# A second residual buffer with rows loaded and biased ahead, and the second norm's rows of thirteen blocks turned on VectorE through DRAM, in a conditioned transformer block

## The chip, the cores and the metric

The kernel runs on one core of one Trainium2 chip. The metric is the device time of one execution in microseconds; a kernel's time is the median of its runs. A profile describes one execution, and its span is a little shorter than that execution's own time.

## The reference, cut to what matters

One transformer block on x (8 x 1024 x 512, fp32), with 16 heads of 32 and an MLP of width 2048. A condition vector for each batch element gives the shifts, scales and gates of the two halves.

```python
mod = silu(condition) @ Wada + bada
sh_a, sc_a, gt_a, sh_m, sc_m, gt_m = jnp.split(mod, 6, axis=1)
xn = _layernorm(x, g1, be1)
xm = xn * (1.0 + sc_a[:, None, :]) + sh_a[:, None, :]
x = x + gt_a[:, None, :] * _attention(xm, Wqkv, Wproj, bproj)   # causal softmax
xn = _layernorm(x, g2, be2)
xm = xn * (1.0 + sc_m[:, None, :]) + sh_m[:, None, :]
h = gelu(xm @ W1 + b1)
x = x + gt_m[:, None, :] * (h @ W2 + b2)
```

## The kernel before

**Blocks and windows.** The tokens are cut into 16 blocks of 512, two for each batch element; block n is the first half of its sequence where n is even and the second, whose queries see twice as many keys, where it is odd. The program is a sequence of windows. In window w TensorE does the attention of block w (scores of four heads at a time, their maxima, exponentials, weights times values) and beside it the "linear" steps that the dictionary `plan` (L231 to L269) lists for that window: the output projection, second norm and MLP of block w-1 (`proj`, `mt`, eight parts `u` and `d`), the v projection of block w, the k and q projections of block w+1, and the loading, first norm and transposition of block w+2 (`load_xa`, `norm_a`, `at`).

**Who decides the order.** All of it is settled while the program is built. A planner keeps estimated times (`now`, `due`, `written`) for each engine and each tile; generators that stand for the linear steps yield what they need, and the planner picks at each point (`work` L1343, `step_aside` L1377) whether attention or a linear step comes next. It also picks VectorE, ScalarE or GpSimd for many small operations (`either` L150, whose VectorE and GpSimd calls are L158 and L161; `combine_out` L192, whose VectorE call is L193; `sooner`). `note` adds to the estimates, and constants such as `LANDING` (10 us) and `HOLDING` (8 us) say when a DMA is expected to be done. Each engine then runs its list in order.

**Products.** The q, k, v, up and down products are seven half-size products each (Strassen-Winograd) and all pass through `matmul` (L197 to L210). Their weights come in pieces of 256 KB through a ring of `RING` = 9 buffers: `fetch` (L328) issues the next load on SyncE as soon as the piece `RING` places earlier is released, and `release` is called when a product is done with its pieces.

**Weights and scores in attention.** Scores go to a PSUM tile, the mask is added (L1531), maxima are taken (L1534), and weights go through the same PSUM tile (L1610) to the exponential (L1622). Where PSUM banks are free the scores of a group are instead made head by head in those.

**Residual rows.** Step `load_xr` (L1258 to L1270) loads the block's 512 rows of x with four DMAs of 256 KB into the one buffer of pool `xrp`; block 14 uses a buffer of the key pool. It stands in the window of that block's projection. `project_out` (L1006) queues four additions of the bias row `gba`, multiplies each projected tile by the gate row `ga`, adds it, and starts the second norm. `down` adds the row `gbm` in its part 0; `settle` adds the MLP's result; `store` (L1100) issues two DMAs of 256 KB for each half block as soon as the last addition is planned, so that SyncE waits at them. `gate_broadcasts` (L508) loads all four rows once for each batch element, each into a tile of its own.

**Norms.** `normalize` (L573) takes statistics on VectorE (L583, L584), makes the reciprocal root and the offset on GpSimd (L605 to L608) and applies them on VectorE or ScalarE (L619, L624) into the tile `hat`, of which there is one. `normalize_tile` (L632) does the same tile by tile in the last block. `modulated` (L685) brings the rows into the transposed layout `xm` and applies gain and shift (L732 VectorE, L738 ScalarE), and then makes sums for Strassen (L746, L748). There are two ways, picked by the set `by_pe` (L375): 16 transposes on TensorE (L728) into PSUM; or `turn` (L656), in which VectorE transposes 32 x 32 squares in four passes (L664), one DMA writes the 1 MB to DRAM (L673), four DMAs read it back with the squares in their places (L678) into `hat`, and the gain and shift read SBUF. Both DMAs are on SyncE's queue, which also carries every weight load; the read-back is issued behind the write and waits until it has landed. Before, all 16 second norms and the first norms of blocks 0 and 1 go through TensorE, and the other 14 first norms are turned.

Of the kernel before, what the change touches and what calls it, by code (L numbers as in the profile page):

```python
# [9 lines left out]
F32 = mybir.dt.float32  # L10
# [12 lines left out]
def kernel(  # L23
# [47 lines left out]
    HB = D // 2  # L71
    RING = 9

# [3 lines left out]
    act = ctx.enter_context(tc.tile_pool(name="act", bufs=2))  # L77
    xrp = ctx.enter_context(tc.tile_pool(name="xrp", bufs=1))
    pp = ctx.enter_context(tc.tile_pool(name="pp", bufs=1))
# [148 lines left out]
    def mlp_steps(n):  # L228
# [6 lines left out]
        0: [("load_xa", 2), ("preps",), ("k", 1), ("norm_a", 2), ("gates", "a"), ("q", 1)]  # L235
        + [("mod", 3), ("at", 2), ("v", 1), ("mod", 4), ("columns_m",), ("gates", "m")],
    }
    late = []
    for w in range(1, NB):
        n = w - 1  # L240
        m = mlp_steps(n)
        even = blocks[n][1] == 0
        rows_a = [("rows", blocks[n][0], "a")] if even else []
        rows_m = [("rows", blocks[n][0], "m")] if even else []
        own = m[:1] + ([("load_xa", w + 2)] if w + 2 < NB else []) + m[1:3]
        own += [("norm_a", w + 2)] if w + 2 < NB else []
        if w == NB - 1:
            steps = late[:1] + [("load_xr", n)] + rows_a + [("proj", n), ("mt", n)] + late[1:]
            steps += [("v", w)] + rows_m + own + m[3:6]
            late = m[6:]  # L250
        else:

            steps = late + [("v", w), ("load_xr", n)] + rows_a + [("proj", n), ("mt", n), ("k", w + 1)]
            if w == 2:
                steps = late + [("v", w), ("k", w + 1), ("load_xr", n)] + rows_a + [("proj", n), ("mt", n)]
            if w == 1:
                steps = [("load_xr", n)] + rows_a + [("k", w + 1), ("proj", n), ("mt", n)]
            steps += [("q", w + 1)] + rows_m + own
            at = [("at", w + 2)] if w + 2 < NB else []
            if blocks[w][1] == 0:  # L260

                steps += m[3:5]
                late = m[5:6] + at + m[6:]
            else:
                steps += m[3:6] + at
                late = m[6:]
        plan[w] = steps
    n = NB - 1
    plan[NB] = [("load_xr", n), late[0], ("beside", late[1]), ("proj", n), ("mt", n)] + mlp_steps(n)  # L269

# [103 lines left out]

    by_pe = {f"m{n}" for n in range(NB)} | {"a0", "a1"}  # L375
    Q = P // NTT
# [20 lines left out]
    make_identity(nc, ident)  # L397
    mask = const.tile([P, 2 * P], F32, tag="mask", name="mask")
    for i in range(2):
        make_causal_mask(nc, mask[:, ts(i, P)], MASKED)  # L400
    eps = const.tile([P, 1], F32, tag="eps", name="eps")
    nc.gpsimd.memset(eps, EPS)
    ones = const.tile([P, P], F32, tag="ones", name="ones")
    nc.gpsimd.memset(ones, 1.0)
# [586 lines left out]

    residual, stored = {}, {}
    y_count, y_keys = [0], {}
# [98 lines left out]
    def settle(n, f, t, y, ky):  # L1092
# [5 lines left out]
        add_to(residual[n][:, half(t, 2), c], y, [ky], keys)  # L1098

    def store(n, t):  # L1100
        b, h = blocks[n]
        for i in (2 * t, 2 * t + 1):
            r0 = h * TB + i * P
            nc.sync.dma_start(out[b, r0 : r0 + P, :], residual[n][:, i, :])
        stored[n + 1] = max(stored.get(n + 1, 0.0), due([("xr", n, 2 * t), ("xr", n, 2 * t + 1)]))

    def down(n, part):
# [85 lines left out]
        if part == 0:  # L1193
            yield [("g", n, 0), ("g", n, 1), "prepared"], []
            for i in range(NTT):
                add_to(residual[n][:, i, :], gate_rows["gbm"], [("row", "gbm")], [("xr", n, i)])
            combine(nc.vector, "B12", "B12", "B11")
# [47 lines left out]
    def perform(step):  # L1245
# [12 lines left out]
        elif kind == "load_xr":  # L1258
            n = step[1]
            b, h = blocks[n]  # L1260
            if n == NB - 2:
                xr = kvp.tile([P, NTT, D], F32, tag="kT", name=f"xr_{n}")
            else:
                xr = xrp.tile([P, NTT, D], F32, tag="xr", name=f"xr_{n}")
            residual[n] = xr
            for t in range(NTT):
                r0 = h * TB + t * P
                nc.sync.dma_start(xr[:, t, :], x[b, r0 : r0 + P, :])
                landed = max(now["PE"], stored.get(n, 0.0)) + LANDING + 700 * t
                written["xr", n, t] = landed  # L1270
        elif kind == "norm_a":
# [179 lines left out]
    def diagonals(parts, sc):  # L1451

        if parts[-1][4] == parts[0][4]:
            first, span = parts[0][3] - P, len(parts) * P
            return span, sc[:, :, first : first + span]
        return 2 * P, sc.rearrange("p j (a c) -> p j a c", c=2 * P)[:, :, :, P:]
# [19 lines left out]
    def scores_by_heads(n, g, parts, reads):  # L1476

        h = blocks[n][1]
        for some in (range(HPG - 1), range(HPG - 1, HPG)):
# [14 lines left out]
            for j, bank in of.items():  # L1494
                if parts[0][1] == h:
                    span, place = diagonals(parts, banks[bank].unsqueeze(1))
                    place = place[:, 0]
                    shape_of = mask[:, :span]
                    if len(place.shape) == 3:
                        shape_of = shape_of.rearrange("p (a c) -> p a c", c=P)  # L1500
                    nc.vector.tensor_tensor(place, place, shape_of, ALU.add)
# [8 lines left out]
    def scores_at_once(n, g, parts, reads):  # L1510
# [149 lines left out]
    def finish(n, g):  # L1660
# [176 lines left out]
    for n in range(NB):  # L1837
        written["attended", n] = NEVER
        written["v done", n] = NEVER
        written["m used", n] = NEVER  # L1840
        if n > 1:
# [73 lines left out]
```

## Time and profile before

| | |
|---|---|
| runs | 3565.46, 3567.45, 3569.86 us; median 3567.45 |
| the profiled execution's own time | 3568.64 us |
| its span | 3566.9 us |
| granted TensorE clock | 0.995 |
| DMA | 461.77 MB, 129 GB/s on average; the main queue holds 43.4% of the 16 engines' time |
| chain of waits | TensorE 88%, DMA 4%, GpSimd 3%, VectorE 3%, ScalarE 1% |

In the lines of the profile PE is TensorE, DVE VectorE, ACT ScalarE, POOL GpSimd and SP SyncE; "SPq" is the queue in which SyncE issues its DMAs. A line of the timeline gives the start of a run of like instructions in us, the us until its last one ends, engine, source line, operation, output<-input, shape and count, and in brackets an idle time ahead of it with what ended it. A line of groups gives the busy us of all of them and the mean ns of one, then the idle time before them. A line of waits gives the instruction that waited, what released it, the us waited in all, the number of waits and the longest. `xm_a`, `hat_a`, `held_a` are the tiles of a first norm, `xm_m`, `hat_m`, `held_m` those of a second one.

### The profile page before, as it was taken

What the parts mean: (1) busy time and instruction counts of PE and PEld (TensorE: products, weight loads), DVE (VectorE), ACT (ScalarE), POOL (GpSimd) and SP (SyncE); (2) the same over time, 40 slices, a digit from 0 to 9 for tenths busy, and PEclk for the clock granted to TensorE, in tenths of its full rate; (3) what the DMA queues carried; (4) which work ended last, traced back from release to release, by engine and by line L of the source; (5) the groups of instructions that cost most, each with busy time, mean ns of one, the idle gap of its engine ahead of it and who ended that gap; (6) DMA issues with size and microseconds to landing.
All of it is one profiled execution on the core that took longest, in us unless ns stands there. A gap on an engine that the chain in (4) does not pass through costs nothing.

```text
span 3566.9 us, 120690 instructions
## 1 busy us (share of the span) xinstructions
PE 3490.9 (98%) x54621; PEld 1741.5 (49%) x54621; DVE 2181.1 (61%) x2395; ACT 1186.3 (33%) x1229; POOL 2081.8 (58%) x2247
## 2 busy tenths in 40 slices
PE   8999999999999999999999999999999999999999
PEld 4444445444554545445454454544545445454445
DVE  6776575665746557365574665746666466665663
ACT  2334333352323514234241442323423134231521
POOL 3667746675456754577536675366762667526660
PEclk9999999999999999999999999999999999999999
DMA  6753434435453344533445334453344533434334
GB/s 201 241 179 93 141 102 127 124 108 155 113 150 107 104 154 117 158 100 101 146 121 148 105 102 146 120 151 103 103 140 126 152 103 105 143 108 142 92 111 137
DMA packets 318259, 461.77 MB, mean 129 GB/s; under 512 B 27052, under 2 KB 177388, under 8 KB 315700
## 3 DMA queue, kind: packets, MB, share of 16 engines
q1 hardware_dynamic: 317632, 454.03, 43.4%
q8 instruction: 430, 7.05, 0.8%
q14 instruction: 81, 0.66, 0.1%
q10 hardware_dynamic: 116, 0.03, 0.0%
HBM read 408.80 MB, written 43.06 MB: 127 GB/s over the span
## 4 chain that ended last, share of the span: by engine, by line
PE 88%; DMA 4%; POOL 3%; DVE 3%; ACT 1%; issue 1%; SPq 1%; ACTq 0%; DVEq 0%; POOLq 0%
PE bank L202 60%; PE sc L1517 8%; PE po L1650 7%; PE st L1610 7%; PE st L1598 3%; DMA w<-in_L_cond_Wproj_dram 2%; PE bank L1671 2%; POOL pT L1740 1%; DMA hat_a<-held_a 1%; PE bank L728 1%; DVE mx L1534 1%; POOL hT L161 1%; PE bank L1572 0%; DVE sc L1531 0%; DMA w<-in_L_cond_Wada_dram 0%
## 5 line engine op out<-in xcount | busy, mean ns | idle before, releaser
L1740 POOL TENSOR_TENSOR pT<-pT,pT 128x256 f32<-128x256 f32 (+3 forms) x1254 | 1213.2, 1003 | 336.1 <-PE po L1650 183.4
L1622 ACT ACTIVATE pT<-st 128x2048 f32<-128x2048 f32 x288 | 541.0, 1878 | 1115.0 <-PE st L1610 1032.9
L202 PE MATMUL bank<-w,hT 128*32 128x256 f32 x14336 | 813.7, 380 | 0.2 <-POOL pT L1627 0.2
L1534 DVE TENSOR_REDUCE mx<-sc 128x4 f32<-128x2048 f32 (+3 forms) x384 | 666.0, 1755 | 216.2 <-PE sc L1517 210.0
L202 PEld LDWEIGHTS bank<-w,hT 128*32 128x32 f32 x14336 | 451.6, 110 | 367.6 <-issue 82.5
L202 PE MATMUL bank<-xm_m,w 128*32 128x256 f32 x8192 | 498.4, 380 | 0.0
L202 PE MATMUL bank<-t_m,w 128*32 128x256 f32 x6144 | 383.2, 380 | 0.1
L202 PEld LDWEIGHTS bank<-xm_m,w 128*32 128x32 f32 x8192 | 256.0, 110 | 222.2 <-issue 55.5
L1627 POOL TENSOR_SCALAR_AFFINE_SELECT pT<-pT 128x512 f32<-128x512 f32 x256 | 169.0, 678 | 332.4 <-ACT pT L1622 332.2
L1517 PE MATMUL sc<-kT,qT 32*128 32x512 f32 (+3 forms) x3072 | 329.1, 520 | 2.0 <-DVE mx L1534 1.7
L1531 DVE TENSOR_TENSOR sc<-sc,mask 128x1024 f32<-128x1024 f32 (+1 forms) x160 | 162.8, 1018 | 273.5 <-PE sc L1517 187.3
L1650 PE MATMUL po<-pT,v 128*32 128x512 f32 (+3 forms) x3048 | 303.1, 493 | 2.0 <-POOL pT L1627 2.0
L1610 PE MATMUL st<-qT,kT 32*128 32x512 f32 (+3 forms) x3072 | 300.6, 487 | 0.0
L202 PEld LDWEIGHTS bank<-t_m,w 128*32 128x32 f32 x6144 | 189.4, 110 | 180.7 <-issue 57.5
L202 PE MATMUL bank<-w,qT 128*32 128x512 f32 x2048 | 244.7, 606 | 21.2 <-DMA w<-in_L_cond_Wproj_dram 19.7
L1689 DVE RECIPROCAL rec<-rec 128x128 f32<-128x128 f32 x256 | 224.5, 919 | 33.2 <-ACT rec L1680 33.2
L202 PE MATMUL bank<-xm_a,w 128*32 128x256 f32 x3968 | 244.6, 380 | 0.0
L1517 PEld LDWEIGHTS sc<-kT,qT 32*128 32x128 f32 x3072 | 129.3, 183 | 172.8 <-ACT pT L1622 63.9
L202 PE MATMUL bank<-t_a,w 128*32 128x256 f32 x2944 | 190.9, 382 | 0.4 <-ACT xm_m L738 0.4
L193 DVE TENSOR_TENSOR hT<-bank,u_u 128x512 f32<-128x512 f32 x192 | 129.3, 685 | 101.2 <-PE bank L202 99.9
L1064 ACT ACTIVATE hT<-hT,cols 128x512 f32<-128x512 f32 x256 | 164.5, 711 | 55.3 <-DVE hT L193 54.7
L202 PEld LDWEIGHTS bank<-xm_a,w 128*32 128x32 f32 x3968 | 123.5, 110 | 106.5 <-issue 30.8
(216 smaller groups left out, 3396.6 us busy)
## 6 DMA issues: line engine op xcount, KB each, us to landing
w<-in_L_cond_W_dram SPq DMA_DIRECT2D x384, 256.0 KB
w<-kept_up_S SPq DMA_DIRECT2D x256, 256.0 KB
w<-kept_down_S SPq DMA_DIRECT2D x256, 256.0 KB
w<-kept_qkv_S SPq DMA_DIRECT2D x180, 256.0 KB
w<-in_L_cond_Wqkv_dram SPq DMA_DIRECT2D x147, 256.0 KB
hat_a<-in_x_dram SPq DMA_DIRECT2D x64, 256.0 KB
w<-in_L_cond_Wproj_dram SPq DMA_DIRECT2D x64, 256.0 KB
xr<-in_x_dram SPq DMA_DIRECT2D x64, 256.0 KB
```

Source lines behind the costliest of these rows:

```text
L193: nc.vector.tensor_tensor(out, src, other, op)
L202: nc.tensor.matmul(ps[r, :], columns, rhs, start=start, stop=stop, skip_group_check=True)
L1064: nc.scalar.activation(hT[:, i, :], hT[:, i, :], AF.Gelu, bias=cols[:, O_B1 + f : O_B1 + f + 1])
L1517: nc.tensor.matmul(sc[:, j, c0 : c0 + w], qTs[n][r, gg, ts(qt, P)], keys_of(n, kh)[r, gg, :w], start=True, stop=True, skip_group_check=True,)
L1531: nc.vector.tensor_tensor(place, place, shape_of.to_broadcast(place.shape), ALU.add)
L1534: nc.vector.tensor_reduce(maxima[n, gg][:, kh, qt, :], sc[:, :, c0 : c0 + w], axis=AX.X, op=ALU.max)
L1610: nc.tensor.matmul(st[:, j, c0 : c0 + w], kT[r, gg, ts(k % NTT, P)], qT[r, gg, TB - w :], start=False, stop=True, skip_group_check=True,)
L1622: nc.scalar.activation(pT[:, :, :used], st[:, :, :used], AF.Exp, scale=scale)
L1627: nc.gpsimd.affine_select(diagonal, diagonal, pattern=[[0, HPG], [1, P]], compare_op=ALU.is_ge, fill=0.0, base=0, channel_multiplier=-1,)
L1650: nc.tensor.matmul(po[r, TB - w :], v[:, k % NTT, g * P + j * hd : g * P + (j + 1) * hd], pT[:, j, c0 : c0 + w], start=(k == 0), stop=last ...
L1689: nc.vector.reciprocal(some, some)
L1740: nc.gpsimd.tensor_tensor(into, into, pT[:, j, c0 : c0 + w], ALU.add)
```

## The change

1. The ring has 8 weight buffers and not 9, and `xrp` has two buffers. The mask is one square and not two, and the tile of ones has 32 columns; the mask addition and the column sums read them by broadcasting or whole.
2. `load_xr` of block w moves from the window of its projection to the window of its attention, behind part 0 of `d` of block w-1 (block 0: into window 0). It is a generator: it waits, in the planner's estimates, until block w-2 is stored, issues two DMAs of 512 KB, waits for the additions to block w-1, loads the bias row and queues the four bias additions. `project_out` waits until that has been done.
3. Bias rows `gba` and `gbm` are loaded for each block (`bias_row`) into one shared tile, `gbm` after the projection; `gate_broadcasts` loads the gate rows alone.
4. `store` is a generator that issues its DMA (one of 512 KB) only once the last addition is planned to be done.
5. `by_pe` keeps a0, a1, m0, m14 and m15, so that the second norms of blocks 1 to 13 go through `turn`.

```diff
-    RING = 9
+    RING = 8
...
-    xrp = ctx.enter_context(tc.tile_pool(name="xrp", bufs=1))
+    xrp = ctx.enter_context(tc.tile_pool(name="xrp", bufs=2))
...
-            steps = late + [("v", w), ("load_xr", n)] + rows_a + [("proj", n), ("mt", n), ("k", w + 1)]
+            steps = late + [("v", w)] + rows_a + [("proj", n), ("mt", n), ("k", w + 1)]
...
-                steps += m[3:5]
+                steps += m[3:5] + [("load_xr", w)]
                 late = m[5:6] + at + m[6:]
             else:
-                steps += m[3:6] + at
+                steps += m[3:5] + [("load_xr", w)] + m[5:6] + at
...
-    by_pe = {f"m{n}" for n in range(NB)} | {"a0", "a1"}
+    by_pe = {"a0", "a1", "m0", f"m{NB - 2}", f"m{NB - 1}"}
...
-    mask = const.tile([P, 2 * P], F32, tag="mask", name="mask")
-    for i in range(2):
-        make_causal_mask(nc, mask[:, ts(i, P)], MASKED)
+    mask = const.tile([P, P], F32, tag="mask", name="mask")
+    make_causal_mask(nc, mask, MASKED)
...
-    ones = const.tile([P, P], F32, tag="ones", name="ones")
+    ones = const.tile([P, hd], F32, tag="ones", name="ones")
...
-        for name in (f"g{kind}", f"gb{kind}"):
-            row = rowp.tile([P, D], F32, tag=f"row{name}", name=f"row_{name}_{b}")
-            nc.sync.dma_start(row, kept_rows[name][b : b + 1, :].to_broadcast([P, D]))
-            gate_rows[name] = row
+        name = f"g{kind}"
+        row = rowp.tile([P, D], F32, tag=f"row{name}", name=f"row_{name}_{b}")
+        nc.sync.dma_start(row, kept_rows[name][b : b + 1, :].to_broadcast([P, D]))
+        gate_rows[name] = row
+
+    def bias_row(n, kind):
+
+        b = blocks[n][0]
+        row = rowp.tile([P, D], F32, tag="rowgb", name=f"row_gb{kind}_{n}")
+        nc.sync.dma_start(row, kept_rows[f"gb{kind}"][b : b + 1, :].to_broadcast([P, D]))
+        gate_rows[f"gb{kind}"] = row
+        written["row", f"gb{kind}", n] = now["PE"] + LANDING
...
-        yield [("attended", n)], []
+        yield [("attended", n), ("xr begun", n)], []
         attT = qTs[n]
         tiles = [residual[n][:, t, :] for t in range(NTT)]
-        for t, xt in enumerate(tiles):
-            xt_job = lambda t=t, xt=xt: add_to(xt, gate_rows["gba"], [("row", "gba")], [("xr", n, t)])
-            pool_jobs.append((xt_job, [("xr", n, t)]))
...
         run_pool_jobs(True)
+        bias_row(n, "m")
...
     def store(n, t):
-        b, h = blocks[n]
-        for i in (2 * t, 2 * t + 1):
-            r0 = h * TB + i * P
-            nc.sync.dma_start(out[b, r0 : r0 + P, :], residual[n][:, i, :])
-        stored[n + 1] = max(stored.get(n + 1, 0.0), due([("xr", n, 2 * t), ("xr", n, 2 * t + 1)]))
+        unstored.setdefault(n, 2)
+
+        def when_added():
+            yield [("xr", n, 2 * t), ("xr", n, 2 * t + 1)], []
+            nc.sync.dma_start(some_rows(out, n, t), residual[n][:, half(t, 2), :])
+            unstored[n] -= 1
+            if unstored[n] == 0:
+                written["stored", n] = now["PE"]
+
+        start(when_added())
+
+    def load_xr(n):
+
+        if n > 1:
+            yield [("stored", n - 2)], []
+        xr = xrp.tile([P, NTT, D], F32, tag="xr", name=f"xr_{n}")
+        residual[n] = xr
+        for t in range(2):
+            nc.sync.dma_start(xr[:, half(t, 2), :], some_rows(x, n, t))
+        for t in range(NTT):
+            written["xr", n, t] = now["PE"] + LANDING
+        if n > 0:
+            yield [("xr", n - 1, t) for t in range(NTT)], []
+        bias_row(n, "a")
+        row = ("row", "gba", n)
+        for t in range(NTT):
+            job = lambda t=t: add_to(xr[:, t, :], gate_rows["gba"], [row], [("xr", n, t)])
+            pool_jobs.append((job, [("xr", n, t), row]))
+        written["xr begun", n] = 0.0
...
         elif kind == "load_xr":
-            n = step[1]
-            b, h = blocks[n]
-            if n == NB - 2:
-                xr = kvp.tile([P, NTT, D], F32, tag="kT", name=f"xr_{n}")
-            else:
-                xr = xrp.tile([P, NTT, D], F32, tag="xr", name=f"xr_{n}")
-            residual[n] = xr
-            for t in range(NTT):
-                r0 = h * TB + t * P
-                nc.sync.dma_start(xr[:, t, :], x[b, r0 : r0 + P, :])
-                landed = max(now["PE"], stored.get(n, 0.0)) + LANDING + 700 * t
-                written["xr", n, t] = landed
+            start(load_xr(step[1]))
...
-            shape_of = mask[:, :span].unsqueeze(1)
-            if len(place.shape) == 4:
-                shape_of = shape_of.rearrange("p o (a c) -> p o a c", c=P)
+            shape_of = mask.unsqueeze(1).unsqueeze(1)
...
-                    banks[bank][r, TB - w :], ones[:, :hd], term[:, j, c0 : c0 + w],
+                    banks[bank][r, TB - w :], ones, term[:, j, c0 : c0 + w],
```

More of the change, by code (lines that the diff above doesn't have):

```diff
@@ L235 @@
         0: [("load_xa", 2), ("preps",), ("k", 1), ("norm_a", 2), ("gates", "a"), ("q", 1)]
-        + [("mod", 3), ("at", 2), ("v", 1), ("mod", 4), ("columns_m",), ("gates", "m")],
+        + [("mod", 3), ("at", 2), ("v", 1), ("load_xr", 0), ("mod", 4), ("columns_m",), ("gates", "m")],
     }
@@ L247 @@
         if w == NB - 1:
-            steps = late[:1] + [("load_xr", n)] + rows_a + [("proj", n), ("mt", n)] + late[1:]
-            steps += [("v", w)] + rows_m + own + m[3:6]
+            steps = late[:1] + rows_a + [("proj", n), ("mt", n)] + late[1:]
+            steps += [("v", w)] + rows_m + own + m[3:5] + [("load_xr", w)] + m[5:6]
             late = m[6:]
         else:
-            steps = late + [("v", w), ("load_xr", n)] + rows_a + [("proj", n), ("mt", n), ("k", w + 1)]
+            steps = late + [("v", w)] + rows_a + [("proj", n), ("mt", n), ("k", w + 1)]
             if w == 2:
-                steps = late + [("v", w), ("k", w + 1), ("load_xr", n)] + rows_a + [("proj", n), ("mt", n)]
+                steps = late + [("v", w), ("k", w + 1)] + rows_a + [("proj", n), ("mt", n)]
             if w == 1:
-                steps = [("load_xr", n)] + rows_a + [("k", w + 1), ("proj", n), ("mt", n)]
+                steps = rows_a + [("k", w + 1), ("proj", n), ("mt", n)]
             steps += [("q", w + 1)] + rows_m + own
@@ L268 @@
     n = NB - 1
-    plan[NB] = [("load_xr", n), late[0], ("beside", late[1]), ("proj", n), ("mt", n)] + mlp_steps(n)
+    plan[NB] = [late[0], ("beside", late[1]), ("proj", n), ("mt", n)] + mlp_steps(n)
     kept_sums = {}
@@ L990, in move_v @@
         vs[n] = v
-    residual, stored = {}, {}
+    residual = {}
     y_count, y_keys = [0], {}
@@ L1098, in settle, with some_rows @@
         add_to(residual[n][:, half(t, 2), c], y, [ky], keys)
-    def store(n, t):
-        b, h = blocks[n]
-        for i in (2 * t, 2 * t + 1):
-            r0 = h * TB + i * P
-            nc.sync.dma_start(out[b, r0 : r0 + P, :], residual[n][:, i, :])
-        stored[n + 1] = max(stored.get(n + 1, 0.0), due([("xr", n, 2 * t), ("xr", n, 2 * t + 1)]))
+    unstored = {}
+    def some_rows(of, n, t):
+        b, h = blocks[n]
+        rows = of[b, h * TB + 2 * t * P : h * TB + (2 * t + 2) * P, :]
+        return rows.rearrange("(t p) d -> p t d", p=P)
+    def store(n, t):
+        unstored.setdefault(n, 2)
[23 more added lines that the diff above has]
+        written["xr begun", n] = 0.0
     def down(n, part):
@@ L1193, in down @@
         if part == 0:
-            yield [("g", n, 0), ("g", n, 1), "prepared"], []
+            yield [("g", n, 0), ("g", n, 1), "prepared", ("row", "gbm", n)], []
             for i in range(NTT):
-                add_to(residual[n][:, i, :], gate_rows["gbm"], [("row", "gbm")], [("xr", n, i)])
+                add_to(residual[n][:, i, :], gate_rows["gbm"], [("row", "gbm", n)], [("xr", n, i)])
             combine(nc.vector, "B12", "B12", "B11")
@@ L1454, in diagonals @@
             first, span = parts[0][3] - P, len(parts) * P
-            return span, sc[:, :, first : first + span]
+            return span, sc[:, :, first : first + span].rearrange("p j (a c) -> p j a c", c=P)
         return 2 * P, sc.rearrange("p j (a c) -> p j a c", c=2 * P)[:, :, :, P:]
@@ L1497, in scores_by_heads @@
                     place = place[:, 0]
-                    shape_of = mask[:, :span]
-                    if len(place.shape) == 3:
-                        shape_of = shape_of.rearrange("p (a c) -> p a c", c=P)
+                    shape_of = mask.unsqueeze(1).to_broadcast(place.shape)
                     nc.vector.tensor_tensor(place, place, shape_of, ALU.add)
@@ L1839 @@
         written["v done", n] = NEVER
+        written["stored", n] = NEVER
+        written["xr begun", n] = NEVER
         written["m used", n] = NEVER
```

## The prediction

> **What bounds the kernel now.** I read the page's busy times first, then TensorE's own waits in the steady part (500 to 3200 us), then SyncE's waits, then the timeline around the steps that the change touches.
>
> ```profile
> span 3566.9 us, 120690 instructions
> PE 3490.9 (98%) x54621; PEld 1741.5 (49%) x54621; DVE 2181.1 (61%) x2395; ACT 1186.3 (33%) x1229; POOL 2081.8 (58%) x2247
> ...
> PE bank L202 <- DMA w<-in_L_cond_Wproj_dram: 19.7, 14, 3.1
> PE bank L202 <- DVE v L193: 5.2, 3, 2.1
> ...
> SPq L1104 <- POOL xr L161: 80.5, 23, 9.0
> ```
>
> TensorE is busy 98% of the span and no other engine passes 61%. So time can come off only by taking instructions from TensorE or by ending its few waits: in the steady part 19.7 us go to pieces of Wproj that land late and 5.2 us to one VectorE step. SyncE stands 80.5 us at output stores whose last addition is not done. That blocks weight loads behind it, but only what shows up as a TensorE wait costs time. A kernel this full also loses time one for one whenever TensorE runs out of work. That is the question of this change.
>
> **The transposes that go.** Block 5's, between two pieces of a projection:
>
> ```profile
> 1316.37 1.06 PE L202 MATMUL bank<-w,qT 128*32 128x512 f32 x8
> 1317.25 1.91 PE L202 MATMUL bank<-xm_a,w 128*32 128x256 f32 x32
> ...
> 1354.08 0.55 PE L728 MATMUL bank<-ident,hat_m 128*128 128x128 f32 x3
> 1354.55 0.64 PE L202 MATMUL bank<-t_a,w 128*32 128x256 f32 x8
> 1355.12 0.76 PE L728 MATMUL bank<-ident,hat_m 128*128 128x128 f32 x5
> 1355.82 1.07 PE L202 MATMUL bank<-t_a,w 128*32 128x256 f32 x16
> 1356.82 1.09 PE L728 MATMUL bank<-ident,hat_m 128*128 128x128 f32 x8
> 1357.84 0.64 PE L202 MATMUL bank<-t_a,w 128*32 128x256 f32 x8
> 1358.35 1.93 PE L202 MATMUL bank<-xm_m,w 128*32 128x256 f32 x32
> 1360.10 1.26 PE L202 MATMUL bank<-t_m,w 128*32 128x256 f32 x20
> ...
> L728 PE MATMUL bank<-ident,hat_m 128*128 128x128 f32 x256 | 44.0, 295 | 4.5 <-ACT hat_m L651 3.4 <-ACT hat_m L624 1.0
> ```
>
> From 1354.08 to 1358.35 pass 4.27 us. In them stand 32 matmuls of a projection, which take 1360.10 - 1358.35 = 1.75 us on their own, so the 16 transposes cost 2.52 us, changes of form included. Thirteen blocks: 13 x 2.52 = 32.8 us. Bounds: the run of eight takes 1357.84 - 1356.82 = 1.02 us, which gives 208 x 0.128 = 27 us; the busy time of the group gives 208 x 44.0 / 256 = 36 us. I take 33 us off. All of it is on the path.
>
> **What comes in on VectorE.** 52 transposes of 32x32 squares, like the first norm's:
>
> ```profile
> L664 DVE STREAM_TRANSPOSE xm_a<-hat_a 128x512 f32<-128x512 f32 x56 | 34.6, 671 | 0.0
> ```
>
> 52 x 0.671 = 34.9 us on an engine that is 39% idle. The gain and shift stay 64 passes, now mostly from SBUF. I cost both at nothing by themselves; the cover is VectorE's idle time. VectorE works in order, though: behind a turn that waits for its rows stand the score maxima, and TensorE's next scores wait for those. I price this inside the next part.
>
> **What comes in as latency.** A turned block cannot start its first MLP product until its rows have gone to DRAM and back. The same route for the first norm, at three places, and its best halves at two:
>
> ```profile
> 125.67 2.43 DVE L664 STREAM_TRANSPOSE xm_a<-hat_a 128x512 f32<-128x512 f32 x4
> 129.23 1.46 SPq L673 DMA_DIRECT2D held_a<-xm_a  x1
> 134.78 3.43 SPq L678 DMA_DIRECT2D hat_a<-held_a  x4
> 144.49 2.91 ACT L738 ACTIVATE xm_a<-hat_a,shifta,gaina 128x512 f32<-128x512 f32 x4
> ...
> 1269.78 2.42 DVE L664 STREAM_TRANSPOSE xm_a<-hat_a 128x512 f32<-128x512 f32 x4
> 1291.67 2.22 ACT L738 ACTIVATE xm_a<-hat_a,shifta,gaina 128x512 f32<-128x512 f32 x3 [3.78 <-DMA hat_a<-held_a]
> ...
> 1703.63 2.42 DVE L664 STREAM_TRANSPOSE xm_a<-hat_a 128x512 f32<-128x512 f32 x4
> 1728.92 2.23 ACT L738 ACTIVATE xm_a<-hat_a,shifta,gaina 128x512 f32<-128x512 f32 x3 [6.96 <-DMA hat_a<-held_a]
> ...
> 2375.30 2.88 SPq L678 DMA_DIRECT2D hat_a<-held_a  x4
> 2383.80 0.82 ACT L738 ACTIVATE xm_a<-hat_a,shifta,gaina 128x512 f32<-128x512 f32 x1 [7.16 <-DMA hat_a<-held_a]
> ```
>
> From the turn's end to the first use: 144.49 - 128.10 = 16.4 us, 1291.67 - 1272.20 = 19.5 us, 1728.92 - 1706.05 = 22.9 us. The best halves, 134.78 - 129.23 = 5.6 out and 2383.80 - 2375.30 = 8.5 back, make 14.1. One modulation (0.8 us of the last row) follows before the first product can start. So 14.9 to 23.7 us. The first norm's trips share the DMA engines with the output stores and the residual loads; the second norm's fall between the projection and the MLP, where only weights move. I take 18, nearer the fast row.
>
> What covers it is TensorE's work between the output projection and the first MLP product. In block 5 the projection ends at 1317.25 and that product starts at 1358.35: 41.1 us. I counted the same stretch in the order of the built programs: 1.75 us a projection piece, the attention groups by their rows. For before this gives 41.6 in block 5, 0.5 too much. For after, W is that work, and E the end of the VectorE turn, both from the end of the output projection. E follows from the place of the turn in VectorE's order. In block 5 it stands behind the fourth product of the q projection:
>
> ```profile
> 1347.36 0.68 DVE L193 TENSOR_TENSOR u_q<-bank,u_q 128x512 f32<-128x512 f32 x1
> ...
> 1342.55 0.20 POOL L608 TENSOR_TENSOR offset_m<-offset_m,rstd_m 128x4 f32<-128x4 f32 x1
> ```
>
> That sum came 1347.36 - 1317.25 = 30.1 us after the projection; by the count of after it is 29.2, then 0.7 for itself and 2.4 for the turn, with the waits between them 32.6. The norm's own scalars (L608, 25.3 us after the projection) are in time for it. All thirteen, in us:
>
> ```
> block    1    2    3    4    5    6    7    8    9   10   11   12   13
> W     29.2 52.7 46.8 46.4 43.6 41.4 42.5 40.1 39.0 42.4 40.2 35.5 40.2
> E     23.7 36.7 39.0 28.2 32.6 19.7 29.1 23.2 20.0 28.2 24.7 19.7 30.3
> idle  12.5  2.0 10.2  0.0  7.0  0.0  4.6  1.1  0.0  3.8  2.5  2.2  8.1
> ```
>
> Idle is E + 18 - W where positive; together 54 us. With 16 it is 35, with 14.9 about 28, with 23.7 some 122. W already holds attention work brought forward: in eleven of the blocks only scores and weights stand between the last q product and the MLP, up to six scores in block 3. Such a stretch cannot run at TensorE's pace:
>
> ```profile
> 1523.77 1.14 PE L1517 MATMUL sc<-kT,qT 32*128 32x512 f32 x8
> ...
> 1528.77 2.29 DVE L1534 TENSOR_REDUCE mx<-sc 128x4 f32<-128x2048 f32 x1 [0.31 <-PE sc L1517]
> 1349.16 1.88 ACT L1622 ACTIVATE pT<-st 128x2048 f32<-128x2048 f32 x1 [2.19 <-PE st L1610]
> ```
>
> Scores and weights share one PSUM tile, so each score holds it for 1.1 us of TensorE and then 2.3 us of VectorE. In block 5, three scores and one weight group between q and the MLP need about 11 us for 5.7 us of TensorE. So even a fast trip leaves about 5 us of idle there.
>
> **Residual rows ahead, stores deferred.** Load, bias additions and stores leave the output projection's neighbourhood. TensorE never waited on the load; SyncE's 80.5 us shrink, since a store now enters its queue only when planned to be ready. Most that this can give TensorE is the 19.7 + 5.2 = 25 us above. Against it stands the weight ring, 8 pieces and not 9: each piece is asked for one product later, 1.75 us, where the Wproj pieces already land late; 14 blocks x 1.75 = 24 us at worst. I take 0 for both together. The queue's own new waits: each trip's write waits for VectorE, its read-back for the write, and behind both stand the weights of the same block's first product, wanted no earlier than the rows. The separate bias rows add 16 loads of 256 KB.
>
> **Sum.** The profiled execution took 3568.64 us, of which 3566.9 are the span; the three runs have a median of 3567.45. 3568.6 - 33 + 54 + 0 = 3590 us.
>
> **The rivals.**
>
> *Trip covered (faster).* Unloaded, the trip takes 14.1 us, the idle is 28, and the Wproj waits go too: 3568.6 - 33 - 20 + 28 = 3544. For it: the best halves were measured beside other traffic. Against it: no single trip of the first norm was that short. By the Trainium skill, "DMA: Bandwidth & Descriptors" (Anatomy of one DMA), a transfer takes about 2 us plus its bytes at 436 GB/s, measured on another issue path; an estimate from it is 4.4 us for each 1 MB way, which would leave idle in block 1 and a little in block 3 alone and some 3545 us in all. Here the rows of this trace show 16.4 to 22.9 us for the two ways, so they do not agree.
>
> *Weights stuck behind the read-back (slower still).* SyncE stands at the read-back until the write has landed, and the second product's weights are issued after it. If they land some 2 us behind the rows in 13 blocks and the trip takes 20.3 us (19.5 and the modulation; idle 80), it is 3568.6 - 33 + 80 + 26 = 3642. This decides once the trip passes some 20 us.
>
> *The change cancels itself.* With a trip of 16 us (idle 35) and no other effect: 3568.6 - 33 + 35 = 3571.
>
> That the transposes stay is no rival: of 256 for the second norm the built program keeps 48.
>
> **How the numbers follow.** Forecast 52%, its own range 3575 to 3625; trip covered 24%; cancelled 10%; weights stuck 14%. A measurement of this kernel tells 0.2%, about 7 us, from no change. Faster by more: 0.25 (the covered trip and a little of the cancelled one); within: 0.10; slower: 0.65. The range runs from 3538, which leaves out about a third of the covered trip's case, to 3632, short of the worst; the sums of the outer bounds (-36 - 25 + 28 and -27 + 24 + 122) lie farther out on both sides.
>
> **What would show it.** Right: TensorE's busy time down by about 30 us; gaps of 2 to 12 us ahead of the first MLP product, largest in blocks 1, 3, 5 and 13 and none in 4, 6 and 9, whose releaser is the modulation and behind it the read-back; trips of 17 to 19 us. Wrong: trips near 14 us or no gaps at those products; a gap in even blocks as large as in odd ones; Wproj waits gone, or doubled by the shorter ring; VectorE, not the trip, as the last releaser.

## The result, and the profile after

The changed kernel takes 3587.45 us (median of four runs, 3585.78 to 3587.63) against 3568.65 us for the kernel before in the same session: a ratio of 1.0052, 95% interval 1.0035 to 1.0070. The prediction said 3590. The sum was close, partly by luck: the idle time came, but not from the cause forecast, and a gain and a loss that the prediction put at nothing nearly cancel.

The page of the kernel after, its own groups, its longest waits of TensorE between 500 and 3200 us, and SyncE's waits:

```profile
span 3585.6 us, 120374 instructions
...
PE 3475.5 (97%) x54413; PEld 1735.1 (48%) x54413; DVE 2189.4 (61%) x2445; ACT 1199.9 (33%) x1252; POOL 2079.6 (58%) x2242
```
```profile
L671 DVE STREAM_TRANSPOSE xm_m<-hat_m 128x512 f32<-128x512 f32 x52 | 33.3, 681 | 0.0
...
L735 PE MATMUL bank<-ident,hat_m 128*128 128x128 f32 x48 | 8.6, 323 | 3.3 <-ACT hat_m L658 3.3
```
```profile
PE st L1620 <- DVE mx L1556: 17.3, 14, 3.8
PE bank L1511 <- DVE mx L1528: 9.4, 5, 2.2
...
PE bank L202 <- DMA w<-in_L_cond_Wproj_dram: 4.3, 5, 1.5
PE bank L202 <- ACT xm_m L745: 3.8, 2, 3.0
```
```profile
SPq L1118 <- POOL xr L161: 30.5, 20, 7.2
```

The transposes fell from 44.0 to 8.6 us, and TensorE has 208 instructions fewer. Yet its busy time fell by 15.4 us only, and the idle rest of the span grew from 76.0 to 110.1. The Wproj waits fell from 19.7 to 4.3 us. What grew is not a wait for the turned rows (`xm_m`: 3.8 us) but for score maxima (`mx`: 17.3 + 9.4 us in the lines shown, 3.6 us before).

**An account of TensorE's time.** From the trace of before I took, for each kind and shape of TensorE work, the median time from the start of a run of like instructions to the start of the next run, per instruction. The sum of these over a stretch is its work; what the stretch took beyond it is its loss: idle time and the slower work at a lower granted clock. A block's path has three stretches: its projection, projection end to first MLP product, and from there to the next projection. Summed over blocks 1 to 13, in us:

```
                 span     work   projection  to the MLP  MLP on  elsewhere
before          3566.9       -      36.6        19.8       3.9     41.2
after           3585.6   -28.9      -0.9        72.1      27.5     50.5
change           +18.7   -28.9     -37.5       +52.3     +23.6     +9.3
```

Only the changes should be read closely. The levels depend on which instructions count as like: told apart by their operands too, the middle column is 2.4 and 55.0, while its change stays at +52.6. Counted directly, TensorE's waits over 0.15 us in that stretch of the thirteen blocks add up to 2.1 us before and 43.5 after, and the time at half clock in it grows from 0 to 29 us, worth at most 14.6.

**Where the 52 us lie.** The end of block 5's stretch in the kernel after: TensorE, then VectorE in the same microseconds, then windows of 5 us (TensorE's busy time follows the length; the third figure from the right is the granted clock).

```profile
1372.76 1.91 PE L202 MATMUL bank<-t_a,w 128*32 128x256 f32 x32
1374.60 1.14 PE L1541 MATMUL sc<-kT,qT 32*128 32x512 f32 x8
1378.16 1.50 PE L1541 MATMUL sc<-kT,qT 32*128 32x512 f32 x8 [2.42 <-DVE mx L1556]
1382.05 0.61 PE L1620 MATMUL st<-mrow,minus_ones 32*128 32x512 bf16 x4 [2.39 <-DVE mx L1556]
1382.43 1.94 PE L1632 MATMUL st<-qT,kT 32*128 32x512 f32 x8
1384.30 1.08 PE L1672 MATMUL po<-pT,v 128*32 128x256 f32 x8
1385.16 1.28 PE L1693 MATMUL bank<-pT,ones 128*32 128x512 f32 x8
1386.45 1.14 PE L1541 MATMUL sc<-kT,qT 32*128 32x512 f32 x8
1387.52 1.93 PE L202 MATMUL bank<-xm_m,w 128*32 128x256 f32 x32
```
```profile
1366.89 2.48 DVE L671 STREAM_TRANSPOSE xm_m<-hat_m 128x512 f32<-128x512 f32 x4
...
1375.81 2.29 DVE L1556 TENSOR_REDUCE mx<-sc 128x4 f32<-128x2048 f32 x1 [0.38 <-PE sc L1541]
1379.71 2.29 DVE L1556 TENSOR_REDUCE mx<-sc 128x4 f32<-128x2048 f32 x1 [1.60 <-PE sc L1541]
1383.39 1.00 DVE L739 TENSOR_SCALAR xm_m<-hat_m,gainm,shiftm 128x512 f32<-128x512 f32 x2 [1.40 <-DMA hat_m<-held_m]
```
```profile
1375.00:1380.00 5.00, 2.24 (x16) 0.41 (x9) 3.02 (x3) 0.00 (x0) 3.15 (x5) 0.88 0.80 204
1380.00:1385.00 5.00, 2.95 (x20) 1.08 (x23) 3.57 (x4) 0.48 (x1) 0.00 (x0) 0.50 0.40 79
1385.00:1390.00 5.00, 4.99 (x68) 2.04 (x64) 2.14 (x5) 3.66 (x5) 1.45 (x2) 0.94 0.00 0
```

The last linear product ends at 1374.6. From there to the MLP at 1387.5 stands only attention: a score waits 2.4 us until VectorE has taken the maxima of the one before, and the weights wait 2.4 us again. By then the granted clock is 0.50, so what follows runs slowly too (the eight `st` products take 1.94 us here, against 1.04 in block 2). The turned rows came back at 1383.4, 14.0 us after the turn's end at 1369.4, and TensorE never stopped for them here. Whether the trip is the cause can't be read from this trace.

### The profile page after: what moved, and what is told of

It is laid out like the page before. It is cut to its first block, busy times and chain, and to the rows that moved or that the text cites. A ratio compares the mean times of both kernels' runs of the same rounds, so it can differ in the third digit from the quotient of the medians.

```text
span 3585.6 us, 120374 instructions
## 1 busy us (share of the span) xinstructions
PE 3475.5 (97%) x54413; PEld 1735.1 (48%) x54413; DVE 2189.4 (61%) x2445; ACT 1199.9 (33%) x1252; POOL 2079.6 (58%) x2242
## 5 line engine op out<-in xcount | busy, mean ns | idle before, releaser
L1556 DVE TENSOR_REDUCE mx<-sc 128x4 f32<-128x2048 f32 (+3 forms) x378 | 652.1, 1746 | 210.6 <-PE sc L1541 204.6
L1541 PE MATMUL sc<-kT,qT 32*128 32x512 f32 (+3 forms) x3024 | 327.6, 522 | 14.4 <-DVE mx L1556 7.7
L1632 PE MATMUL st<-qT,kT 32*128 32x512 f32 (+3 forms) x3072 | 309.2, 492 | 0.0
L1736 POOL TENSOR_TENSOR qT<-top,rec 128x512 f32<-128x512 f32 x61 | 81.2, 1332 | 196.7 <-DVE rec L1711 175.0
```

What stands on the lines that cost most here:

```text
L1541: nc.tensor.matmul(sc[:, j, c0 : c0 + w], qTs[n][r, gg, ts(qt, P)], keys_of(n, kh)[r, gg, :w], start=True, stop=True, skip_group_check=True,)
L1556: nc.vector.tensor_reduce(maxima[n, gg][:, kh, qt, :], sc[:, :, c0 : c0 + w], axis=AX.X, op=ALU.max)
L1632: nc.tensor.matmul(st[:, j, c0 : c0 + w], kT[r, gg, ts(k % NTT, P)], qT[r, gg, TB - w :], start=False, stop=True, skip_group_check=True,)
L1736: nc.gpsimd.tensor_tensor(qTs[n][:, g, :], top, rec, ALU.mult)
```

## The experiments

Each was compared with the kernel before on the same chip; medians of that lay between 3564.1 and 3566.4 us. Where a fence shows waits of TensorE, they are those between 500 and 3200 us.

### The two halves apart

Rows and stores of the change, without the turn:

```diff
-    by_pe = {"a0", "a1", "m0", f"m{NB - 2}", f"m{NB - 1}"}
+    by_pe = {f"m{n}" for n in range(NB)} | {"a0", "a1"}
```

> The changed kernel with all sixteen second norms turned by TensorE again; two residual buffers, rows loaded and biased ahead, stores deferred and the ring of 8 stay. Theory A, from the account of TensorE's idle time in the two traces (208 transposes -33, idle ahead of the first MLP product +52, waits inside the projections -37, short waits elsewhere +24): the waits inside the projections belong to the rows and stores, so 3531 if the 24 us of short waits belong to the turned rows, 3555 if they belong to the shorter ring or the rows. Rival B, the prediction's own term: rows and ring together give 0, 3568. The waits at pieces of Wproj should be under 6 us by A, about 20 by B.

Measured: 3544.04 us, ratio 0.9947 (0.9934 to 0.9959). The projections' loss is 7.5 us, that behind the first MLP product 2.5. So this half gains 22 us, and B falls. 3544 lies between A's two figures.

The turn of blocks 1 to 13 alone, the reverse edit in the kernel before:

> The kernel before with only the second norms of blocks 1 to 13 turned on VectorE; ring of 9, one residual buffer, four residual loads beside the projection. Theory A: 3568.6 - 33 + 52 = 3588, and 3612 if the 24 us of short waits belong to the turn; the waits at Wproj stay near 20 us. Rival C: it was the turn, by changing the order, that ended the projection's waits; then 3550 to 3575 with the Wproj waits gone.

Measured: 3623.96 us, ratio 1.0172 (1.0157 to 1.0187), longer than theory A's 3612. The loss ahead of the MLP is 91.1 us, that behind it 33.1. Both short-wait terms belong to the turn. The waits at Wproj did fall, to 7.3 us, and the projections' loss by some 20 us, so C's effect exists, but the other losses outweigh it. On top of the rows' half the turn costs 1.0052 - 0.9947, about 1.05% or 37 us; alone 1.7%. Why it costs more alone wasn't tried.

The kernel before with `RING = 8`:

> The kernel before with a ring of 8 weight buffers and nothing else. The prediction's bound: up to +24 us, 3592, with longer waits at Wproj. Theory A: the loads run far enough ahead that the ninth buffer is worth little: 3568 to 3575.

Measured: 3571.80 us, ratio 1.0017 (1.0009 to 1.0026): about 6 us for the ninth buffer, not 24.

### Is it the trip?

The trip taken out, with every engine's order kept (the rows are then not in their places, so this kernel leaves out what the turn is for):

```diff
-        nc.sync.dma_start(held, small_blocks)
+        if key[0] == "a":
+            nc.sync.dma_start(held, small_blocks)
...
-            nc.sync.dma_start(rows[ts(m, Q), :, :], some)
+            if key[0] == "a":
+                nc.sync.dma_start(rows[ts(m, Q), :, :], some)
```

> The changed kernel, with the write of the turned second-norm rows to DRAM and their read-back left out, so that gain and shift are applied to rows that are not in their places; the planner's estimates and so the order of every engine stay as they are. Theory A (the trip of some 17 us is what the idle time ahead of the first MLP product consists of): that idle falls from 72 us to under 20, time 3530 to 3540. Rival D (VectorE's place for the turn, or the scores that cannot run at TensorE's pace in that stretch, sets it): idle stays above 45 us, time 3560 to 3580.

Measured: 3584.06 us, ratio 1.0056 (1.0044 to 1.0069). Theory A as I had written it falls: without the DMAs of the trip the loss ahead of the MLP is 71.8 us instead of 72.1. Of rival D the idle time came true, and the time lies 4 us above its range; D leaves open whether VectorE or the order of the scores sets it. The same place of block 5 in that kernel:

```profile
1377.21 1.14 PE L1543 MATMUL sc<-kT,qT 32*128 32x512 f32 x8
1380.77 1.14 PE L1543 MATMUL sc<-kT,qT 32*128 32x512 f32 x8 [2.41 <-DVE mx L1558]
1384.32 0.61 PE L1622 MATMUL st<-mrow,minus_ones 32*128 32x512 bf16 x4 [2.41 <-DVE mx L1558]
...
1390.44 1.93 PE L202 MATMUL bank<-xm_m,w 128*32 128x256 f32 x32
```

The two waits of 2.4 us are still there. They stand in TensorE's order, and that order was made for a trip that the planner takes to last 2 x `HOLDING` = 16 us. So I formed theory F: the planner, not the DMA, lays the idle time down. Its rival G keeps VectorE and its place for the turn. The next two runs change what the planner is told. First no trip, and the planner knows it:

```diff
-        written["held", key] = now["PE"] + HOLDING
+        written["held", key] = now["PE"] + (HOLDING if key[0] == "a" else 0)
...
-        written["turned", key] = now["PE"] + HOLDING
+        written["turned", key] = now["PE"] + (HOLDING if key[0] == "a" else 0)
```

> The changed kernel without the write to DRAM and the read-back of the second norm's turned rows (gain and shift are applied to rows that are not in their places), as in turn_without_trip, but with the planner told that the rows are ready at once, so that it may put the first MLP product directly behind the turn. Theory F (the idle time ahead of that product is laid down by the planner: it expects 16 us of trip, has no linear work left, and fills the time with attention that waits for its own maxima): that idle falls from 72 us to 20-25 as in the kernel with the rows ahead alone, time 3544 - 33 = 3511 to 3525. Rival G (it is VectorE's turn and its place, or the other layout of the rows, that costs): time stays above 3560.

Measured: 3531.92 us, ratio 0.9906 (0.9893 to 0.9919). The loss ahead of the MLP is 14.4 us, less than F said, and G falls; the time is 7 us above F's range, for which see the losses behind the MLP below. In block 5 the last product of q is now followed at once by the MLP:

```profile
1348.78 1.05 PE L1674 MATMUL po<-pT,v 128*32 128x384 f32 x16
1349.65 0.61 PE L202 MATMUL bank<-xm_a,w 128*32 128x256 f32 x8
1350.08 1.91 PE L202 MATMUL bank<-xm_m,w 128*32 128x256 f32 x32
```

A trip of some 16 us in the planner's estimate is thus worth 72 - 14 = 58 us of loss, and 1.0052 - 0.9906 of the time, 52 us. Second, the trip as it is, with 4000 in place of 0 in those two lines:

> The changed kernel with the trip as it is, but the planner told that each way of it takes 4 us and not 8. Theory F: the planner calls the MLP some 8 us earlier, the stretch holds less attention, and TensorE now waits for the read-back itself (waits whose releaser is the modulation of xm_m or its sums): the idle time changes its name, not its size; 3575 to 3610. Rival H (the planner's estimate was too long for a trip of some 17 us): 3550 to 3570.

Measured: 3608.41 us, ratio 1.0124 (1.0109 to 1.0138); the loss ahead of the MLP is 76.7 us. Now TensorE does stop for the rows:

```profile
PE bank L202 <- ACT xm_m L745: 30.1, 6, 9.7
PE st L1620 <- DVE mx L1556: 11.0, 12, 3.8
```

Theory F holds, and H falls. The planner may let TensorE wait for the trip openly, or fill it with attention that waits for itself.

### Work that needs no attention

If so, more linear work behind the projection should end the loss. The v projection of a window is moved behind the output projection:

```diff
-            steps = late + [("v", w)] + rows_a + [("proj", n), ("mt", n), ("k", w + 1)]
+            steps = late + rows_a + [("proj", n), ("mt", n), ("v", w), ("k", w + 1)]
...
-                steps = late + [("v", w), ("k", w + 1)] + rows_a + [("proj", n), ("mt", n)]
+                steps = late + [("v", w)] + rows_a + [("proj", n), ("mt", n), ("k", w + 1)]
```

> The changed kernel with the v projection of a window moved from ahead of the output projection to behind it, which puts seven more products, 12.3 us of work that needs no attention, between the projection and the first MLP product of blocks 1 to 13 (block 1: in place of k, which stood ahead). Theory F: the idle time ahead of that product falls from 72 us to under 30, time 3535 to 3550. Rival G: no fall, 3575 or more. A loss elsewhere is possible: weights times values wait for v about 7 us longer.

Measured: 3557.73 us, ratio 0.9980 (0.9971 to 0.9989). The loss ahead of the MLP is 12.2 us, as F says; the time is 8 us above its range. One of the losses elsewhere is a single wait of 12.0 us for an attention quotient, in block 11's projection:

```profile
PE bank L202 <- POOL qT L1736: 14.0, 3, 12.0
```

The same move with no block turned:

> The same move of v with all second norms turned by TensorE, as in rows_ahead_alone. It is the control for v_behind_projection: theory F expects no gain here, 3540 to 3550, since no trip has to be covered; if the move gains as much here as there, it isn't the cover.

Measured: 3541.88 us, ratio 0.9936 (0.9924 to 0.9949), against 3544.04 without the move. So what the move gains in the turned kernel (1.0052 - 0.9980, 26 us) is the cover. But the covered turn (3557.73) is 16 us slower than no turn at all, though it saves 33 us of transposes. The loss behind the first MLP product takes 24 of them back (33.4 us against 9.3), and the projections another 16, chiefly block 11's wait and the slow clock behind it.

Is the loss behind the first MLP product VectorE's extra 33 us of work? In the kernel without a trip, the 52 VectorE transposes were left out as well:

```diff
-            nc.vector.transpose(into, rows[:, t, :].rearrange("p (h m i) -> p h m i", m=NTT, i=Q))
+            if key[0] == "a":
+                nc.vector.transpose(into, rows[:, t, :].rearrange("p (h m i) -> p h m i", m=NTT, i=Q))
```

> As no_trip_planned (3532), with the 52 VectorE transposes of second-norm rows left out as well, while the planner still counts them, so that every engine's order stays as it is; gain and shift are applied to rows that are not transposed. That kernel saved 33 us of TensorE and is only 12 us faster than rows_ahead_alone. Theory J (the missing 21 us are waits for a VectorE that has 35 us more to do and delivers score maxima later): 3512 to 3518. Theory K (they lie in the order that the planner makes, with less work between attention groups): 3528 to 3534.

Measured: 3529.29 us, ratio 0.9901 (0.9887 to 0.9914), against 3531.92. Theory J falls, in this kernel at least: the 33 us on VectorE cost next to nothing. The loss stays with the order (30.3 us behind the MLP, 29.3 with the transposes). With the transposes, waits over 0.15 us make up 17 us of it in blocks 1 to 13, most of them about 1 us, the longest 3.1. What the rest consists of, and which choice of the planner makes the waits, wasn't tried.

They are mostly in even blocks: in v_behind_projection's trace the even blocks 4, 6, 8 and 12 lose 3.8, 2.8, 4.5 and 8.8 us behind the MLP, the odd ones 3 to 11 at most 1.2 (block 13 is an exception, with 4 to 5). So only the odd blocks were turned, with v moved:

```diff
-    by_pe = {"a0", "a1", "m0", f"m{NB - 2}", f"m{NB - 1}"}
+    by_pe = {f"m{n}" for n in range(NB) if n % 2 == 0 or n == NB - 1} | {"a0", "a1"}
```

> As v_behind_projection, but only the odd blocks 1 to 13 turned on VectorE; the even ones go through TensorE. From that run's account: the idle time ahead of the MLP is about 0.2 us in odd blocks, and the short waits behind it 0 to 1.5 us there against 3 to 9 in even ones. Theory F: 7 x 2.5 us of transposes saved less some 5 us of waits, against 3542 with no block turned: 3528 to 3536. Rival I (short waits come with each turned block wherever it stands, about as much as its transposes cost): 3540 to 3550.

Measured: 3525.14 us, ratio 0.9889 (0.9874 to 0.9905), the fastest kernel of this study and faster than both that it started from; it is 3 us below F's range, and rival I falls. Against 3541.88 with no block turned, 17 us are gained for 7 x 2.5 = 17.5 us of transposes. In block 5 linear work now stands right up to the first MLP product:

```profile
1349.63 1.15 PE L1541 MATMUL sc<-kT,qT 32*128 32x384 f32 x16
1350.71 1.50 PE L202 MATMUL bank<-t_a,w 128*32 128x256 f32 x24
1352.03 1.91 PE L202 MATMUL bank<-xm_m,w 128*32 128x256 f32 x32
```

### Where the rows' half gains

The stores issued as in the kernel before, in the kernel with the rows ahead:

```diff
-        def when_added():
-            yield [("xr", n, 2 * t), ("xr", n, 2 * t + 1)], []
-            nc.sync.dma_start(some_rows(out, n, t), residual[n][:, half(t, 2), :])
...
+        for i in (2 * t, 2 * t + 1):
+            r0 = h * TB + i * P
+            nc.sync.dma_start(out[b, r0 : r0 + P, :], residual[n][:, i, :])
...
+            written["stored", n] = due([("xr", n, i) for i in range(NTT)])
```

> As rows_ahead_alone (3544), but the output stores are issued as in the kernel before: two of 256 KB for each half block, as soon as the last addition is planned, so that SyncE stands at them until it is done. Theory S (the waits inside the projections came from stores that held up the weight loads behind them): Wproj waits return to 20 us or more and the time to 3560-3566. Theory L (they came from the 1 MB of residual rows loaded right beside the Wproj pieces): Wproj waits stay near 8 us, time 3544 to 3550.

Measured: 3588.68 us, ratio 1.0063 (1.0050 to 1.0075): 1.16% or 41 us above rows_ahead_alone by the ratios, more than theory S had said. The projections' loss is 43.8 us. The waits of TensorE and SyncE here, and then those in rows_ahead_alone:

```profile
PE bank L202 <- DMA w<-in_L_cond_Wproj_dram: 34.1, 18, 4.1
```
```profile
SPq L1118 <- POOL xr L161: 87.7, 21, 9.1
```
```profile
PE bank L202 <- DMA w<-in_L_cond_Wproj_dram: 8.1, 11, 1.4
```
```profile
SPq L1118 <- POOL xr L161: 16.6, 15, 6.7
```

Moving the loads without deferring the stores is no gain but a loss of 22 us against the kernel before, so theory L falls; 7 us of that loss lie in the projections (43.8 against 36.6), the ring of 8 may hold some 6, and the rest stays unexplained. The other way round, deferred stores with one residual buffer and a ring of 9:

```diff
-        if n > 1:
-            yield [("stored", n - 2)], []
-        xr = xrp.tile([P, NTT, D], F32, tag="xr", name=f"xr_{n}")
+        if n > 0 and n != NB - 2:
+            yield [("stored", n - 2 if n == NB - 1 else n - 1)], []
+        if n == NB - 2:
+            xr = kvp.tile([P, NTT, D], F32, tag="kT", name=f"xr_{n}")
+        else:
+            xr = xrp.tile([P, NTT, D], F32, tag="xr", name=f"xr_{n}")
```

> All second norms by TensorE, ring of 9 and ONE residual buffer (block 14 in the key pool's), the rows loaded where the kernel before loads them, in two DMAs and only after the block before is stored; the stores deferred until their additions are planned to be done, bias rows loaded for each block. Theory S (all of the gain of the rows' half is that SyncE no longer stands at stores): Wproj waits 10 us or less, 3538 to 3548. Rival M (deferred stores need the second buffer, since the loads of the next rows, their landing and their bias additions now come after the stores and just ahead of the projection): waits of projections or of their neighbours for residual rows, 3555 to 3590.

Measured: 3543.86 us, ratio 0.9936 (0.9921 to 0.9952), the same as with two buffers and a ring of 8, with this row:

```profile
PE bank L202 <- DMA w<-in_L_cond_Wproj_dram: 1.7, 4, 0.8
```

Theory S holds. The second buffer and the early loads with a ring of 8 give no more than one buffer and a ring of 9. In every run a deferred store is one of 512 KB and a store issued at once two of 256 KB; the size wasn't tried alone. That SyncE stands 87.7 us at stores issued at once and 16.6 at deferred ones speaks for the deferring.

## Why the prediction was right, and where it was not

**The transposes, -33.** Right. From start to start their group went from 44.4 to 11.8 us, and the account's work fell by 28.9, since other forms changed a little.

**The trip, 18 us.** Too long. From the turn's end to the first use of the rows and 0.8 us the thirteen blocks take 12.5 to 19.7 us, 17.2 on average. But that is mostly where the planner put the first use: in turn_without_trip, with no DMA to wait for, the same interval is 15.9 on average, and in the kernel after the first use is seen to wait for the read-back in five blocks only. In hold_4us it waits for it in all thirteen, and there the trip takes 12.5 to 17.3 us, 14.3 on average.

**The idle time it leaves, +54.** The loss has about that size (+52.3), and its place by blocks is near: I had the most in blocks 1, 3, 13 and 5, and they lose 11.7, 11.0, 7.0 and 7.5 us. But the waits in it are only 41 us more than before; the rest is mostly half clock, for which the sum had no term. The step that failed is "idle is E + 18 - W where positive", with TensorE stopped at the MLP and the read-back as its releaser. Removing the DMAs did not move that idle time; telling the planner that there is no trip removed it. The ends of the turn came within 4 us of my E, and what follows them is the planner's 16 us, filled with attention. That my 18 lay near this constant is luck: with 16 the same formula gives the 35 us named in the prediction, and with the 14.3 of hold_4us 24. My remark that such a stretch "cannot run at TensorE's pace", put in as a floor of 5 us, was the mechanism. It fits block 2, forecast at 2.0 us and losing 8.9: it has the longest stretch of all (W 52.7), and its four waits of 1.1, 2.4, 0.8 and 1.0 us all stand at scores or weights.

**Rows ahead, deferred stores and the ring, 0.** Wrong in size: -22 together, of which the ring is about +6. I took the gain to be 25 us at most, the named waits of TensorE, and let 24 us for the ring cancel it. The waits understate the loss. Block 7's projection in the kernel before:

```profile
1729.89 1.07 PE L202 MATMUL bank<-w,qT 128*32 128x512 f32 x8 [2.54 <-DMA w<-in_L_cond_Wproj_dram]
1731.82 3.33 PE L202 MATMUL bank<-w,qT 128*32 128x512 f32 x16 [0.86 <-DMA w<-in_L_cond_Wproj_dram]
```
```profile
1730.00:1735.00 5.00, 4.14 (x28) 0.91 (x31) 3.05 (x5) 1.15 (x2) 1.78 (x1) 0.72 0.96 320
```

The waits are 3.4 us, and the clock of 0.72 takes another 5 x 0.28 = 1.4; the account has 5.1 us of loss there. Over thirteen blocks it has 36.6 us, all of which went in the kernel after.

**What was not forecast.** The losses behind the first MLP product, +23.6, and elsewhere, +9.3. They and the projections' -37.5 nearly cancel, and that is why 3590 came so near to 3587. The forecast total was right for a reason that is only half the one given.

**The signs named.** Of those for being wrong three were seen: Wproj waits nearly gone (4.3 us), a loss in block 2 above that of blocks 5 and 13, and VectorE as the last releaser. Of those for being right, TensorE's busy time fell by 15.4 us and not 30, since half clock lengthens what is left, and the releasers were others.

**The rivals.** Of weights stuck behind the read-back nothing is seen: the trip did not pass 20 us, and TensorE's only waits for weights between 500 and 3200 us are the 4.3 us at Wproj. The covered trip had the better trip time (14.9 against 14.3 in hold_4us), but there the loss is 76.7 us and not 28; it needs v moved to be covered. The "some 3545 us" in that rival comes to 3568.6 - 33 + 6 = 3542 when redone from E and W.

## What to carry to other kernels

A transposition that leaves the busiest engine for a DMA trip has to be paid with work that can run without waiting, not just with any work that is ready; count the independent products between the two ends before making the trip, and look at what the new order loses behind it: here that loss decided which blocks to turn. A store that is issued before its data are ready holds up the loads behind it in the queue; here issuing it later was worth the same with one residual buffer as with two. When a scheduler fills a gap, take the latency out of the kernel and out of the scheduler's estimate separately: the first alone can show nothing. And a time from producer to consumer is a transfer's time only where the consumer waits for it.

## What the runs showed of the hardware

Short gaps can slow TensorE afterwards. In block 5 of the kernel after a gap of 2.42 us ends at 1378.16, and the granted clock (third figure from the right, in windows of 1 us) falls before the next gap begins at 1379.66:

```profile
1377.00:1378.00 1.00, 0.00 (x0) 0.00 (x0) 1.00 (x1) 0.00 (x0) 1.00 (x2) 1.00 0.67 137
1378.00:1379.00 1.00, 0.84 (x8) 0.41 (x9) 0.10 (x1) 0.00 (x0) 0.15 (x1) 0.90 0.90 264
1379.00:1380.00 1.00, 0.66 (x4) 0.00 (x0) 0.29 (x1) 0.00 (x0) 0.00 (x0) 0.50 1.09 215
```

It stays at 0.50 until 1385 us. In block 8 of the same trace a single gap of 2.42 us, which ends at 2026.94, leaves 0.50 from 2028 to 2030; in block 2 one of 2.41 us, which ends at 714.97, leaves the clock at 1.00. In block 7 of the kernel before, the clock is still 1.00 behind a gap of 2.54 us and falls only after one of 0.86 us that follows it, to 0.72 over 5 us. What decides between these cases no run here shows. The mean clock fell from 0.995 to 0.991 with the change, which is up to 0.004 x 3586 = 14 us of its 18.7 (less, so far as it fell while TensorE was idle). The Trainium skill, "TensorE: Matmul & The Clock Gate" (What's actually happening), states half rate after at least one idle window of about 3.4 us; here single gaps of 2.42 us were enough.
